# Layer 3's first high parts in layer 2's places, and whole rows' table rows read in pieces

## The chip, the cores and the metric

The kernel runs on one core of a Trainium2 chip. The metric is the device time of one execution in microseconds (us); lower is better. The engines named below are TensorE (PE; its weight loads are PEld), VectorE (DVE), ScalarE (ACT), GpSimd (POOL) and SyncE (SP), which issues most loads and stores.

## What is computed

Four graph layers over 2708 nodes with 512 features. The change touches the end of layer 2 and all of layer 3:

```python
h = jnp.maximum(_layernorm(x), 0.0)
h = relu(adj @ (h @ W1) + b1)             # layer 2, first pass
h = relu(adj @ (h @ W3) + b3)             # layer 2, second pass
x = x + tanh(h @ Wf + bf)

h = jnp.maximum(_layernorm(x), 0.0)       # layer 3
A = (adj != 0)
hidden = h @ W + b                        # 2708 x 512: "the table"
x = x + (A @ hidden) / A.sum(axis=0)[:, None]
```

The adjacency matrix is sparse: its density falls with the node number in both directions, so the first nodes have many neighbours and the last ones few.

## The kernel before

**Tiles.** Nodes are cut into 22 tiles of 128 (the last has 20), and "row m" is the work for the 128 outputs of node tile m. The first six tiles of neighbours (`DENSE = 6`) are taken whole by every row. Of the other 16 a row takes only the neighbours that occur, as lists of 128 found in layer 0: row m has `CHUNKS[m]` of them (9 for row 2, 8 for row 3, 7 for rows 4 to 7, then 6 and 5, and 2 for the short row 21). One indirect DMA of 256 KB on POOL gathers the 128 table rows of one list. Rows 0 and 1 are so dense that layer 3 takes all 22 tiles of neighbours for them ("full rows", `FULL = (0, 1)`).

**Layer 2's second pass** goes over rows 0, 6 to 21, and then 1 to 5. Each row aggregates (lines 946 and 949), projects with `Wf`, applies tanh, adds the residual, normalises, projects with `W`, and stores its part of the table to DRAM as `hid` (line 1240), and from row 6 on to `hidr` as well, from which layer 3 gathers. The six dense tiles' right-hand sides stay in SBUF in three forms, `ghi0..5`, `glo0..5` and `gs0..5`. `gs0` becomes the residual of row 5, the last one.

**Layer 3's ordinary rows** are 2 to 20, with row 21 in the middle (`order_3`). A row's sum is a chain of matmuls into one PSUM bank, of a 0/1 mask on the left and a part of the table on the right. Every table tile is split in two parts that together hold its full precision: a high part by a copy on ACT (line 1073), and a low part by a subtraction on DVE, in place (line 1075). So each tile or list costs two matmuls.

- `hidden(t)` loads dense tile t of the table into `glo{t}` (line 1084) and splits it, with the high part in `ghi{t}`. Both places come free when layer 2's last row has aggregated.
- `gather_h(m)` loads row m's marks (line 1118) and issues its gathers (line 897). Their places come from `room()`: four in `wr`, then eight `gg` places and four of a `wb` weight in turn. Row 2 has the four `wr` places and five `gg`; row 3 three `gg`, four `wb` and one `gg`; row 4 seven `gg`. The `wb` tiles hold the weights of the last projection with `W`.
- `whole_h(m, t0, t1)` makes masks from the marks, three tiles at a time (line 1146), and issues the products with dense tiles t0 to t1.
- `listed_products(m)` makes the lists' masks (line 1157), splits the gathered parts and issues their products. The places of the high parts come from `part_room()`: `v_hi`, `v_lo` and `v_s` in turn, two of each. These are also the places in which layer 2's projections keep the three forms of their left-hand sides.
- `finish_h(m)` scales, adds the residual and stores (lines 1169 and 1172).

Three rows are begun ahead (`AHEAD = 3`): products with the dense tiles 0 to 4 are issued for rows 2, 3 and 4 before any list, and those with tile 5, which layer 2 computes last, behind the row's list. After that every row finishes and starts the one three further on.

**The full rows** are done in steps, one after each ordinary row from the third on: two steps with the dense tiles, six (`others`) with three further table tiles each, and that for rows 0 and 1. These further products are of full-precision operands, not of halves; their table tiles are read by `load_full()`, 16 loads of up to 256 KB (line 1180) into `wa0`, `wa1`, `wa2` and `wr`, issued together in the code after the first ordinary row. The adjacency piece of each step is loaded at line 880 and turned into a 0/1 mask on DVE (line 1191 for dense tiles, 1198 for others).

**Order.** Each engine runs its instructions in a fixed order. The code gives each instruction its priority; a planner makes each engine's order when the kernel is built, taking instructions whose inputs and places it expects to be free by then. So an instruction can run long before its neighbours in the code.

Of the kernel before, what the change touches and what calls it, by code (L numbers as in the profile page):

```python
# [9 lines left out]
FP = mybir.dt.float32  # L10
FR = mybir.dt.float32r
# [11 lines left out]
P = 128  # L23
# [13 lines left out]
DENSE = 6  # L37
# [5 lines left out]
def kernel(  # L43
# [27 lines left out]
    nc = tc.nc  # L71

    N, D = x.shape
    H, _, DK = wk_d.shape
    NT = (N + P - 1) // P
    NFULL = N // P
    TAIL = N - NFULL * P
    NCD = D // P
# [8 lines left out]
    def rows(t):  # L87
        return min(P, N - t * P)

    def dense_of(m):  # L90

        return 0 if m == NT - 1 else DENSE
# [15 lines left out]
    hid = dram.tile([N + 1, D], FP, name="hid")  # L108
# [42 lines left out]
    def span(t):  # L151
        return slice(t * P, t * P + rows(t))
# [8 lines left out]
    def load_w(pool, src, name):  # L161
        w = pool.tile([P, NCD, D], FP, name=name)
        nc.sync.dma_start(out=w, in_=src.rearrange("(c p) k -> p c k", p=P))
        return w

    def norm(pool, xt, n, dst, func=AF.Identity):

        stats = pool.tile([P, nc.vector.BN_STATS_DIM], FP, name="stats")
        nc.vector.bn_stats(stats[:n], xt[:n])
        mv = pool.tile([P, nc.vector.BN_AGGR_DIM], FP, name="mv")  # L170
        nc.vector.bn_aggr(mv[:n], stats[:n])
        rstd = pool.tile([P, 1], FP, name="rstd")
        nc.scalar.activation(rstd[:n], mv[:n, 1:2], AF.Sqrt, bias=eps[:n])
        nc.vector.reciprocal(rstd[:n], rstd[:n])
        shift = pool.tile([P, 1], FP, name="shift")
        nc.vector.tensor_scalar(
            shift[:n], mv[:n, 0:1], rstd[:n], -1.0, op0=ALU.mult, op1=ALU.mult
        )
        nc.scalar.activation(dst[:n], xt[:n], func, scale=rstd[:n], bias=shift[:n])
# [30 lines left out]
    wset = short.enter_context(tc.tile_pool(name="wset", bufs=1))  # L210
# [6 lines left out]
    with tc.tile_pool(name="l0_slab", bufs=2) as slabs, tc.tile_pool(  # L217
        name="l0_h", bufs=1
    ) as hp, tc.tile_pool(name="l0_w", bufs=2) as wp, tc.tile_pool(
        name="l0_acc", bufs=2, space=PSUM  # L220
    ) as ps_acc, tc.tile_pool(name="l0_small", bufs=1, space=PSUM) as ps_small, tc.tile_pool(
        name="l0_list", bufs=3, space=PSUM
    ) as ps_list, tc.tile_pool(name="l0_tr", bufs=1, space=PSUM) as ps_tr, tc.tile_pool(
        name="l0_y", bufs=1, space=PSUM
# [504 lines left out]
        for m in range(NT):  # L729
# [44 lines left out]
            if m == NT // 2 + 2:  # L774
                wr = load_w(wset, w1_d, "wr")
                w1 = split_w(wset, wr, "wa")
                wr = load_w(wset, w3_d, "wr")
# [12 lines left out]
    gp = short.enter_context(tc.tile_pool(name="g", bufs=1))  # L790
    wsetb = short.enter_context(tc.tile_pool(name="wsetb", bufs=1))
    ap = short.enter_context(tc.tile_pool(name="ap", bufs=2))
# [78 lines left out]
    PIECE = 3  # L871
    dense = [list(range(t, min(t + PIECE, DENSE))) for t in range(0, DENSE, PIECE)]
    others = [list(range(t, min(t + PIECE, NFULL))) for t in range(DENSE, NFULL, PIECE)]
# [119 lines left out]
    xs, ys, g1, g1p = {}, {}, {}, {}  # L993
    AHEAD = 9

    def fetch(t):

        n = rows(t)
        xs[t] = gp.tile([P, D], FP, name=f"slot{t % AHEAD}")
        nc.sync.dma_start(out=xs[t][:n], in_=x1[t][:n])  # L1000
        ys[t] = gp.tile([P, D], FP, name=f"slot{AHEAD + t % AHEAD}")
        nc.gpsimd.indirect_dma_start(
            out=ys[t][:n],
            out_offset=None,
            in_=y[:, :],
            in_offset=bass.IndirectOffsetOnAxis(ap=idx[:n, t : t + 1], axis=0),
        )

    def first_product(t):
# [6 lines left out]
        norm(wp, xt, n, hn)  # L1016
        if t + AHEAD < NT:
            fetch(t + AHEAD)
        banks = (ps_a, ("agg", "aggs")) if t % 2 else ()
# [13 lines left out]

    for t in range(min(AHEAD, NT)):
        fetch(t)
    w3 = split_w(wsetb, wr, "wb")
    wr = load_w(wset, wf_d, "wr")

    for m in order_m:
        n = rows(m)  # L1040
        parts = aggregated(m, first_parts, first_product, g1d, bias1, marked=True)
        if m == 0:
            wf = split_w(wset, wr, "wa")
            wr = load_w(wset, w_d, "wr")
# [43 lines left out]
    def room():  # L1088


        quad = wset.tile([P, NCD, D], FP, name="wr")
        for c in range(NCD):
            yield quad[:, c, :]
        i = 0
        while True:
            for _ in range(NGG):
                yield gathered()
            quad = wsetb.tile([P, NCD, D], FP, name=f"wb{i % 3}")
            i += 1
            for c in range(NCD):  # L1100
                yield quad[:, c, :]

    places_h, part_slot = room(), [0]

    def part_room():
        name = ("v_hi", "v_lo", "v_s")[part_slot[0] % 3]
        part_slot[0] += 1
        return wp.tile([P, NCD, P], FR, name=name).rearrange("p c k -> p (c k)")


# [26 lines left out]
    def products_of(m):  # L1137
        return 2 * (dense_of(m) + CHUNKS[m])

    def whole_h(m, t0=0, t1=DENSE):  # L1140

        n = rows(m)
        t1 = min(t1, dense_of(m))
        for ts in (range(t, min(t + PIECE, t1)) for t in range(t0, t1, PIECE)):
            mask = ap.tile([P, PIECE, P], FR, name="a_hi" if t1 - t0 > 1 else "a_s")
            nc.vector.tensor_copy(
                mask[:, : len(ts), :n], marks[m][:, ts[0] : ts[-1] + 1, :n]
            )
            for i, t in enumerate(ts):
                for half in hidden(t):  # L1150
                    add_h(m, mask[:, i, :n], half, products_of(m))

    def listed_products(m):
        n = rows(m)
        whole, num = dense_of(m), CHUNKS[m]
        mask = ap.tile([P, NCA, P], FR, name="ac")[:, :num, :n]
        nc.scalar.copy(mask, marks[m][:, whole : whole + num, :n])
        for c, g in enumerate(listed_h.pop(m)):
            for half in split_h(part_room(), g, P):
                add_h(m, mask[:, c, :], half, products_of(m))  # L1160
# [12 lines left out]

    full_h = {}

    def load_full():
        for i, t0 in enumerate(range(DENSE, NT, NCD)):
            quad = wset.tile([P, NCD, D], FP, name=("wa0", "wa1", "wa2", "wr")[i])
            for t in range(t0, min(t0 + NCD, NT)):
                nc.sync.dma_start(out=quad[: rows(t), t - t0, :], in_=hid[span(t)])  # L1180
                full_h[t] = quad[:, t - t0, :]

    def full_steps(m, name):

        n = rows(m)
        total = 2 * DENSE + sum(map(len, others))
        banks[m] = ps_p.tile([P, D], FP, name=name)
        for t0 in range(0, DENSE, PIECE):
            mask, k = load_piece(m, list(range(t0, t0 + PIECE)))
            high = ap.tile([P, PIECE, P], FR, name="a_lo")  # L1190
            nc.vector.tensor_scalar(high[:, :, :n], mask, 0.0, None, op0=ALU.not_equal)
            for i in range(PIECE):
                for half in hidden(t0 + i):
                    add_h(m, high[:, i, :n], half, total)
            yield
        for ts in others:
            mask, k = load_piece(m, ts)
            nc.vector.tensor_scalar(mask, mask, 0.0, None, op0=ALU.not_equal)
            for i, t in enumerate(ts):
                add_h(m, mask[:k, i, :n], full_h[t][:k], total)  # L1200
            yield
        finish_h(m)


    order_3 = [m for m in range(NT) if m not in FULL and m != NFULL]
# [44 lines left out]


    steps = in_steps()
    AHEAD = 3
    for k in order_3[:AHEAD]:
        if k not in marks:
            gather_h(k)
        whole_h(k, 0, DENSE - 1)
    for i, m in enumerate(order_3):
        listed_products(m)
        if i < AHEAD:  # L1260
            whole_h(m, DENSE - 1)
        finish_h(m)
        if i == 0:
            load_full()
        if i + AHEAD < len(order_3):
            k = order_3[i + AHEAD]
            gather_h(k)
            whole_h(k)
        if i > 1:
            next(steps, None)  # L1270
        if i == 1:
            some = wp.tile([P, 1], FP, name="some", bufs=1)
            nc.vector.tensor_reduce(some, bad, AX.X, ALU.add)
            tot = ps_t.tile([P, 1], FP, name="pt")
            nc.tensor.matmul(tot, ones, some, start=True, stop=True)
            nc.vector.tensor_scalar_min(some, tot, 1.0)
            nc.vector.tensor_copy(flag, some)
# [8 lines left out]
    with tc.If(general > 0):  # L1286

        with tc.tile_pool(name="l0_g", bufs=2) as gp, tc.tile_pool(
            name="l0_gh", bufs=1
# [9 lines left out]
            for m in range(NT):  # L1299
# [23 lines left out]
                for t in range(NT):  # L1323
                    k = rows(t)
# [18 lines left out]
        with tc.tile_pool(name="l1_qkv", bufs=1) as qkvp:  # L1343
# [6 lines left out]
            with tc.tile_pool(name="l1_pw", bufs=1) as pwp, tc.tile_pool(  # L1350
                name="l1_ph", bufs=2
            ) as php, tc.tile_pool(name="l1_px", bufs=3) as pxp, tc.tile_pool(
                name="l1_pps", bufs=2, space=PSUM
# [4 lines left out]
                for w, src in ((wk, wk_d), (wq, wq_d), (wv, wv_d)):  # L1358
                    for h in range(H):
                        nc.sync.dma_start(  # L1360
                            out=w[:, :, h * DK : (h + 1) * DK],
                            in_=src[h].rearrange("(c p) k -> p c k", p=P),
# [34 lines left out]
            with tc.tile_pool(name="l1_bias", bufs=2) as bp, tc.tile_pool(  # L1397
                name="l1_p", bufs=2
            ) as pp, tc.tile_pool(name="l1_pT", bufs=3) as ptp, tc.tile_pool(
                name="l1_x", bufs=1  # L1400
            ) as xp, tc.tile_pool(name="l1_st", bufs=4) as stp, tc.tile_pool(
                name="l1_s", bufs=2, space=PSUM
            ) as ps_s, tc.tile_pool(name="l1_t", bufs=2, space=PSUM) as ps_t, tc.tile_pool(
                name="l1_o", bufs=1, space=PSUM
            ) as ps_o, tc.tile_pool(name="l1_y", bufs=1, space=PSUM) as ps_y:
                SW = 2 * BLK
                for m in range(NT):
# [11 lines left out]
                    for h in range(H):  # L1419
# [23 lines left out]
                        for t0 in range(0, NT, 4):  # L1443
                            ts = range(t0, min(t0 + 4, NT))
                            pt = ps_t.tile([P, 4, P], FP, name="pt")
                            pT = ptp.tile([P, 4, P], FP, name="pT")
                            for t in ts:
                                k = rows(t)
# [9 lines left out]
                            for t in ts:  # L1458
                                k = rows(t)
# [29 lines left out]
        with ExitStack() as gen:  # L1489
# [8 lines left out]
            gp = l2.enter_context(tc.tile_pool(name="g", bufs=2))  # L1498
# [213 lines left out]
```

## Time and profile before

| | us |
|---|---|
| median of 7 runs | 1485.69 (1481.43 to 1491.27) |
| the profiled execution | 1490.49 |
| its span, first to last instruction | 1488.7 |
| PE / DVE / ACT / POOL busy in the span | 1305.7 / 940.1 / 676.9 / 668.4 |
| layer 3's gathers on POOL (all places) | 120, at a median of about 0.95 each |
| ACT cast to a high part, line 1073 | 0.62 |
| DVE subtraction, line 1075 | 0.69 |

The profiled execution lies 4.8 us above the median and within the range of the runs. A busy PE is not PE at its peak; the granted clock has to be read beside it. In the timelines below, a row gives the start, the duration (for several instructions in one row their whole stretch), the engine, the line, the operation, destination and source by the program's names with buffer numbers left out, the count, and in brackets the engine's idle time before it and what ended that.

### The profile page before, as it was taken

To read this page: it belongs to the slowest core of one execution; us is meant where nothing else is said; L and a number is where in the kernel's file an instruction comes from. 1 tells how busy PE (TensorE), PEld (TensorE's weight loads), DVE (VectorE), ACT (ScalarE), POOL (GpSimd) and SP (SyncE) were. 2 spreads that over 40 slices of the span, in tenths; PEclk is the share of its full clock that TensorE was granted. 3 is DMA by queue.
4 is the path that set the end of the run, shared out by engine and by line. 5 is a ranking of instruction groups with operands and counts; after the bars stand their busy time and mean duration, and the time that the engine had idled before them with its cause. 6 is when DMAs were issued, how large, how long until landed. Compare 5 with 4: busy or idle time off the path is not lost. (4 is left out here: it accounts for less than half of the span.)

```text
span 1488.7 us, 15398 instructions
## 1 busy us (share of the span) xinstructions
PE 1305.7 (88%) x4400; PEld 771.6 (52%) x4400; DVE 940.1 (63%) x1888; ACT 676.9 (45%) x1040; POOL 668.4 (45%) x690
## 2 busy tenths in 40 slices
PE   5487889779778769989999999899999999778997
PEld 2133334334333346656656666465676666456664
DVE  2578877978879679543334446465666665565664
ACT  5998545453111256432232335244445444454543
POOL 1263667556553332055544441334424345157762
PEclk9699999889889879999999999999999999879998
DMA  8999999887696497378776777756555666478874
GB/s 290 330 342 310 336 309 308 298 254 214 207 327 226 145 316 246 103 228 268 246 234 210 237 228 229 247 158 196 177 172 161 209 198 205 122 245 260 265 238 143
DMA packets 195941, 351.27 MB, mean 236 GB/s; under 512 B 26445, under 2 KB 107693, under 8 KB 192114
## 3 DMA queue, kind: packets, MB, share of 16 engines
q1 hardware_dynamic: 148453, 200.68, 40.3%
q0 software_dynamic: 47392, 149.51, 32.1%
q8 instruction: 37, 0.61, 0.2%
q14 instruction: 59, 0.48, 0.1%
HBM read 286.99 MB, written 63.12 MB: 235 GB/s over the span
## 5 line engine op out<-in xcount | busy, mean ns | idle before, releaser
L949 PE MATMUL aggs<-gg,ac 128*128 128x512 f32 (+1 forms) x520 | 232.5, 595 | 4.6 <-DMA gg<-g1d,idx_g 4.6
L897 POOL DMA_INDIRECT gg<-g2d,idx_g x130 | 130.9, 1007 | 218.4 <-PE aggs L949 169.2
L897 POOL DMA_INDIRECT gg<-g1d,idx_g x130 | 132.4, 1019 | 176.5 <-PE aggs L949 106.0
L741 PE MATMUL acc<-h,inc 128*128 128x512 f32 x348 | 168.5, 627 | 26.5 <-DVE inc L600 23.9
L532 POOL DMA_INDIRECT ac<-in_adj_t_dram,idx_a x130 | 130.6, 1004 | 87.8 <-issue 32.6
L949 PEld LDWEIGHTS aggs<-gg,ac 128*128 128x128 f32 (+1 forms) x520 | 97.8, 189 | 111.2 <-issue 101.0
L550 POOL DMA_INDIRECT h<-h0d,idx_g x111 | 111.7, 1006 | 90.4 <-PE acc L741 66.6
L741 PEld LDWEIGHTS acc<-h,inc 128*128 128x128 f32 x348 | 66.0, 199 | 105.9 <-issue 70.5
L946 PE MATMUL agg<-ghi,a_hi 128*128 128x512 f32 x252 | 115.6, 459 | 3.0 <-ACT a_hi L933 2.7
L933 ACT ACTIVATE a_hi<-raw 128x384 fp32r<-128x384 f32 x84 | 43.5, 519 | 163.1 <-issue 86.7
L741 PE MATMUL acc<-h,incl 128*128 128x512 f32 (+1 forms) x222 | 105.3, 621 | 0.0
L946 PE MATMUL agg<-glo,a_lo 128*128 128x512 f32 x252 | 102.1, 405 | 1.5 <-ACT glo L200 1.5
L946 PE MATMUL aggs<-gs,a_s 128*128 128x512 f32 x252 | 100.6, 402 | 0.7 <-DVE gs L197 0.6
L897 POOL DMA_INDIRECT gg<-hidr,idx_h x79 | 78.6, 995 | 48.6 <-PE agg L1133 16.9
L934 DVE TENSOR_TENSOR a_lo<-raw,a_hi 128x384 fp32r<-128x384 f32 x84 | 47.3, 563 | 77.9 <-ACT a_hi L933 51.2
L157 PE MATMUL yacc<-wvo,hT 128*128 128x512 f32 (+1 forms) x176 | 87.4, 643 | 4.6 <-ACT hT L186 4.5
L843 DVE SCALAR_TENSOR_TENSOR v_lo<-pt,v_hi 128x512 fp32r<-128x512 f32 (+1 forms) x88 | 56.6, 664 | 45.9 <-ACT v_hi L842 45.3
L824 DVE SCALAR_TENSOR_TENSOR u<-aggs,u 128x512 f32<-128x512 f32 x42 | 28.9, 687 | 77.2 <-PE aggs L949 75.6
L741 PEld LDWEIGHTS acc<-h,incl 128*128 128x128 f32 (+1 forms) x222 | 43.5, 199 | 53.8 <-issue 51.6
L483 ACT ACTIVATE sgn<-ar 128x2708 bf16<-128x2708 f32 (+1 forms) x22 | 54.0, 2454 | 35.7 <-DMA ar<-in_adj_dram 35.2
L842 ACT ACTIVATE v_hi<-pt 128x512 fp32r<-128x512 f32 (+1 forms) x88 | 48.6, 578 | 43.9 <-PE pt L837 41.8
L514 DVE FIND_INDEX8 at_top<-top,ar 128x8 uint32<-128x2708 f32 (+1 forms) x22 | 65.3, 2969 | 0.0
(275 smaller groups left out, 2774.2 us busy)
## 6 DMA issues: line engine op xcount, KB each, us to landing
ar<-in_adj_dram SPq DMA_DIRECT2D x27, 1354.0 KB
raw<-in_adj_t_dram SPq DMA_DIRECT2D x108, 192.0 KB
slot<-x SPq DMA_DIRECT2D x41, 256.0 KB
at<-in_adj_t_dram SPq DMA_DIRECT2D x27, 384.0 KB
ranks<-rank_b SPq DMA_DIRECT2D x20, 485.0 KB
ac<-lst SPq DMA_DIRECT2D x16, 384.0 KB
h<-in_x_dram SPq DMA_DIRECT2D x21, 256.0 KB
h0d<-h POOLq DMA_DIRECT2D x21, 256.0 KB, 6.0
```

The lines of the kernel that those rows point to most:

```text
L157: nc.tensor.matmul(acc[:n], hT[:, c, :n], w[:, c, :], start=(c == 0), stop=(c == NCD - 1))
L483: nc.scalar.activation(sgn[:n], ar[:n], AF.Sign, accum_out=sum_sgn[:n])
L514: nc.vector.max_index(at_top[:n], top[:n], ar[:n])
L532: nc.gpsimd.indirect_dma_start(out=ac[:, c, :n], out_offset=None, in_=adj_units, in_offset=bass.IndirectOffsetOnAxis(ap=idx_a[:, m, c0 + c ...
L550: nc.gpsimd.indirect_dma_start(out=g, out_offset=None, in_=h0d[:, :], in_offset=bass.IndirectOffsetOnAxis(ap=idx_g[:, m, c : c + 1], axis=0),)
L741: nc.tensor.matmul(acc[:n], a, g, start=(i == 0), stop=(i == len(pairs) - 1))
L842: nc.scalar.activation(hi[d], pt[d], AF.Relu, scale=UP)
L843: nc.vector.scalar_tensor_tensor(lo[d], pt[d], 0.0, hi[d].bitcast(FP), op0=ALU.max, op1=ALU.subtract)
L897: nc.gpsimd.indirect_dma_start(out=gs[c], out_offset=None, in_=gd[:, :], in_offset=bass.IndirectOffsetOnAxis(ap=index[:, m, c : c + 1], ax ...
L934: nc.vector.tensor_tensor(lo[d], raw, hi[d].bitcast(FP), ALU.subtract)
L946: nc.tensor.matmul(acc[:n], a[:k, i, :n], b[:k], start=st, stop=sp)
L949: nc.tensor.matmul(mixed[:n], a, g, start=(c == 0 and not dense_of(m)), stop=(c == len(chunks) - 1),)
```

## The change

Four edits.

1. `part_room()`: the first 14 high parts (nine of row 2, five of row 3) go to `gs1` to `gs5` in turn. From then on every other part goes there and the others to `v_hi`, `v_lo` and `v_s`, so that there are eleven places instead of six.
2. Row 2's listed products come first of layer 3, ahead of any product with a dense tile. For the other rows they stay where they were.
3. For the first three rows the dense tiles 4 and 5 are late, instead of tile 5 alone (`LATE = 2`). The name of the mask follows: `a_s` for the late piece, `a_hi` otherwise.
4. `load_full(ts)` is called by the full rows' steps: each asks for its own table tiles and the next step's, if they aren't there yet. The places are as before.

```diff
+    NFIRST = 14
+
     def part_room():
-        name = ("v_hi", "v_lo", "v_s")[part_slot[0] % 3]
+        i = part_slot[0]
         part_slot[0] += 1
+        if i < NFIRST or i % 2:
+            return gp.tile([P, D], FR, name=f"gs{1 + (i if i < NFIRST else i // 2) % (DENSE - 1)}")
+        name = ("v_hi", "v_lo", "v_s")[i // 2 % 3]
         return wp.tile([P, NCD, P], FR, name=name).rearrange("p c k -> p (c k)")
...
-            mask = ap.tile([P, PIECE, P], FR, name="a_hi" if t1 - t0 > 1 else "a_s")
+            mask = ap.tile([P, PIECE, P], FR, name="a_s" if t0 else "a_hi")
...
-    def load_full():
-        for i, t0 in enumerate(range(DENSE, NT, NCD)):
-            quad = wset.tile([P, NCD, D], FP, name=("wa0", "wa1", "wa2", "wr")[i])
-            for t in range(t0, min(t0 + NCD, NT)):
-                nc.sync.dma_start(out=quad[: rows(t), t - t0, :], in_=hid[span(t)])
-                full_h[t] = quad[:, t - t0, :]
+    quads = {}
+
+    def load_full(ts):
+        for t in ts:
+            i, j = divmod(t - DENSE, NCD)
+            if t in full_h:
+                continue
+            if i not in quads:
+                name = ("wa0", "wa1", "wa2", "wr")[i]
+                quads[i] = wset.tile([P, NCD, D], FP, name=name)
+            full_h[t] = quads[i][:, j, :]
+            nc.sync.dma_start(out=full_h[t][: rows(t)], in_=hid[span(t)])
...
-        for ts in others:
+        for j, ts in enumerate(others):
+            load_full(sum(others[j : j + 2], []))
             mask, k = load_piece(m, ts)
...
-    AHEAD = 3
-    for k in order_3[:AHEAD]:
+    AHEAD, LATE = 3, 2
+    for i, k in enumerate(order_3[:AHEAD]):
         if k not in marks:
             gather_h(k)
-        whole_h(k, 0, DENSE - 1)
+        if i == 0:
+            listed_products(k)
+        whole_h(k, 0, DENSE - LATE)
     for i, m in enumerate(order_3):
-        listed_products(m)
+        if i:
+            listed_products(m)
         if i < AHEAD:
-            whole_h(m, DENSE - 1)
+            whole_h(m, DENSE - LATE)
         finish_h(m)
-        if i == 0:
-            load_full()
```

## The prediction

> **What bounds the kernel now.** I read the page first, then a table of busy time by stage, then the timelines of TensorE (PE), ScalarE (ACT), SyncE (SP) and GpSimd (POOL) around the seam between layer 2's last row and layer 3, since every edit lies there or later. The page's chain of waits covers only the last 17 us and tells nothing of the change. The page's first line:
>
> ```profile
> PE 1305.7 (88%) x4400; PEld 771.6 (52%) x4400; DVE 940.1 (63%) x1888; ACT 676.9 (45%) x1040; POOL 668.4 (45%) x690
> ```
>
> PE is the fullest engine, but an average hides where it isn't. Stages of layer 3 (stage, its length, busy us of PE, PEld, DVE, ACT, POOL, granted clock, DMA share, GB/s):
>
> ```profile
> 1300.00:1314.00 14.00, 7.54 (x22) 5.36 (x23) 6.96 (x15) 7.06 (x11) 0.00 (x0) 0.63 0.73 248
> 1314.00:1330.00 16.00, 10.92 (x49) 8.68 (x48) 10.49 (x18) 9.13 (x17) 12.62 (x12) 0.97 0.76 250
> 1330.00:1345.00 15.00, 12.32 (x41) 9.65 (x41) 8.06 (x17) 7.39 (x14) 11.34 (x13) 0.80 0.80 242
> 1345.00:1375.00 30.00, 26.64 (x97) 19.89 (x98) 18.34 (x33) 13.12 (x22) 23.30 (x23) 0.92 0.82 256
> 1375.00:1437.00 62.00, 59.98 (x219) 40.57 (x217) 41.97 (x77) 30.95 (x54) 46.32 (x47) 0.98 0.87 276
> ```
>
> From 1375 PE is 97% busy and sets the pace. Between 1300 and 1375 PE is busy 57.4 of 75 us, and POOL does nothing before 1314. The hole is there. PE's waits in it (start, length, idle before and its releaser in brackets):
>
> ```profile
> 1306.46 0.79 PE L1133 MATMUL agg<-ghi,a_hi 128*128 128x512 f32 x1 [6.75 <-ACT ghi L1073]
> ...
> 1330.15 0.80 PE L1133 MATMUL agg<-ghi,a_s 128*128 128x512 f32 x1 [5.23 <-ACT ghi L1073]
> ...
> 1371.34 0.50 PE L1133 MATMUL aggs<-v_lo,ac 128*128 128x512 f32 x1 [2.18 <-ACT v_lo L1073]
> ```
>
> The first two wait for table tiles 4 and 5, the last to be computed; the third for a gathered row. ACT shows what held them:
>
> ```profile
> 1305.79 0.62 ACT L1073 CAST ghi<-glo 128x512 fp32r<-128x512 f32 x1 [3.89 <-DMA glo<-hid]
> ...
> 1328.96 0.62 ACT L1073 CAST v_lo<-gg 128x512 fp32r<-128x512 f32 x1 [2.81 <-DMA gg<-hidr,idx_h]
> 1329.48 0.61 ACT L1073 CAST ghi<-glo 128x512 fp32r<-128x512 f32 x1
> ```
>
> Tile 4 waits for its own load. Tile 5's cast has no idle time: it stands in ACT's queue behind a cast that waited for a gather. SP:
>
> ```profile
> 1301.31 0.32 SPq L1084 DMA_DIRECT2D glo<-hid  x1
> 1301.73 4.38 SPq L1180 DMA_DIRECT2D wa<-hid  x8
> ...
> 1317.88 1.28 SPq L1180 DMA_DIRECT2D wr<-hid  x3
> 1320.10 0.32 SPq L1084 DMA_DIRECT2D glo<-hid  x1
> ```
>
> Tile 4's load (`glo<-hid`) follows four of `load_full`'s 256 KB loads and took 4.5 us (1301.31 to 1305.79); two earlier ones, issued at 1267.54 and 1284.63, took 2.7 and 2.6. Tile 5's follows three more. POOL:
>
> ```profile
> 1275.55 0.95 POOL L897 DMA_INDIRECT gg<-hidr,idx_h  x1 [0.30 <-issue]
> 1314.02 1.33 POOL L897 DMA_INDIRECT wb<-hidr,idx_h  x1 [37.52 <-issue]
> ...
> 1366.14 0.95 POOL L897 DMA_INDIRECT gg<-hidr,idx_h  x1 [0.30 <-PE main L1133]
> ```
>
> POOL idles 37.5 us: its next place is `wb`, the weights of the last row's last product. Then it issues 40 gathers to the one at 1366.14, 52.1/39 = 1.34 us apart, and that one's landing (about 1370.7) ends PE's third wait. So 1314 to 1371 is a chain of POOL issues.
>
> **What the Trainium skill says.** "Perfetto Trace Analysis", Tensor Engine Instruction, says that ACT, DVE and GpSimd are strict first-in first-out; the cast at 1329.48 agrees. "DMA: Bandwidth & Descriptors", Queues, rings and completion order, says that descriptors are taken in ring order within a queue and that an engine takes turns between queues; the 4.5 against 2.6 us agree. "TensorE: Matmul & The Clock Gate", Part 1, says that an idle window of about 3.4 us halves the clock; after each of the two long waits the matmuls start 0.43 us apart instead of 0.23.
>
> **The change, part by part.** *The order on each engine.* It is planned when the kernel is built, and the planner moves ready work far ahead: layer 3's first marks load (L1118) runs at 891.8, before layer 2's second pass, and two of the third stage's pieces are already turned into masks (L1198) at 1273 and 1275, 90 us before their use at 1364. I assume the same afterwards.
>
> *Table rows in pieces.* The same 16 loads, no byte less. Twelve go to `wa`, free at 1297.9, and SP has nothing else to send: later in the code is not later in time here. I take them as unmoved: 0. If they do move, tile 4 lands in 2.6 instead of 4.5 us: -1.9; and the first of the steps, which then asks for six rows (1.5 MB, at the 250 GB/s shown 6 us), could wait up to +4. The four in `wr` can start once row 2's first four products are done, now before the seam: they leave tile 5's way. On SP they then stand ahead of row 4's or 5's store of `hid`: if PE comes to row 2 later than planned, that store waits with them; bounds 0 and +2, I take 0.
>
> *Row 2's listed products first, in the places of layer 2's right-hand sides.* They move 9 casts (0.62), 9 subtractions (0.69) and 18 matmuls. `gs1` to `gs5` are last read at 1265.85 (L946); row 2's gathers, the last of them issued at about 1272, land by 1277; the mask is cast at 1256. Today the casts start at 1311.31, when `v_hi` to `v_s` come free of the last row. Now all fits before 1306. PE: 18 x 0.23 = 4.1 us into the waits of 6.75, 2.68 and 1.28 us at 1299, 1285 and 1290: hidden. With five places for nine parts, the sixth cast waits for PE's first product, and behind it on ACT wait the last row's casts and activations. On ACT and DVE all 18 stand among the last row's own steps. I take two casts on its path, +1.0; bounds 0 and +4.5, where one casts waits for a gather's landing (4.5 median) ahead of a step of the row. The filled wait keeps the clock up for the last row's matmuls: -0.5 (ten matmuls between 1306.5 and 1312 started 0.43 apart, 2 us, of which little is on the path).
>
> *POOL's head start.* Row 2 frees five `gg` places. They are those of row 3's last gather and row 4's first four, so five gathers go into the 37.5 us in which POOL idles and come out of the chain behind 1314: 5 x 1.34 = -6.7. If row 3's first three products, whose gathers have landed too and which are among the first 14 parts, also run before 1314, three more go: -10.7. I take -6.7, since these stand behind the late tiles in the code.
>
> *LATE = 2.* Tile 4's products move behind row 2's list for all three first rows. Today row 4's mask for tiles 0 to 2 waits for a place held until tile 4 arrives (masks at 1308.02 and 1308.87); with tile 3 alone in the second piece, row 4's 8 matmuls can fill the first wait too. No instruction is added: the late mask covers two tiles instead of one. 26 x 0.23 = 6.0 us of cover against 6.75. Counted with POOL, since PE has slack: 0; bounds -2 and 0.
>
> *Tile 5's wait.* 5.23 us plus the slow matmuls after it are PE slack before 1371, not a second gain: the gathers end last there. Less traffic by the `wr` loads shortens the landings (5.2 us for that of 1323.71 against 4.5): -0.7.
>
> *Eleven places for parts instead of six, later.* ACT can cast five parts further ahead. From 1375 PE is the bound and a part that is ready sooner gains nothing; 0, bounds -3 (PE's idle time after 1375 on parts) and +14 (below).
>
> Sum: 1.0 - 0.5 - 6.7 - 0.7 = -6.9, call it -7. From 1371 on PE carries the lead to the end: the same products follow in the same order. The profiled execution took 1490.49 us around a span of 1488.7, so it would take about 1483.5; it lies 4.8 above the median of 1485.69, and from that the change gives 1478.7.
>
> **Rivals.** *A, more is gained: 1472.* Eight gathers move, tile 4's wait shrinks: -10.7 - 1.9 - 0.7 = -13. For it: PE's slack between 1300 and 1371, about 17.6 us, allows it. Against: needs row 3 early.
>
> *B, the loads really spread: 1476.* -7 - 1.9, minus or plus the step's wait. Against it: the marks at 891.8.
>
> *C, the lead is lost: 1484.* The planner still sends the `wb` gathers first, as now (seven of them at 1314), and row 4's wait behind them; or the lead is spent at the next place: row 7's last `gg` places are freed by row 6's products, and from 1358.56 on most `gg` gathers are released by PE, not by POOL itself. Only the landings and a part of the seam stay: -2.
>
> *D, slower: 1493.* ACT and DVE, first-in first-out, park at gathers of rows further ahead, and masks, subtractions and finishes of nearer rows stand behind. Between 1314 and 1375 ACT already waits 19.2 us for gathers, and PE's waits for masks (`a_hi`) are 8.0 us in 5, 1.6 each. With eleven places the plan lets ACT pass the point where six now hold it. One such wait in every second of 18 rows is 0.8 x 18 = 14.4, less the 7. It cancels the gain from 0.39 us a row, and makes the kernel slower by 4.5 us from 0.64. Against: in PE's stage gathers land ahead of need, and PE's longest wait for a part there is 0.53 us.
>
> **How the numbers follow.** Forecast 0.42, A 0.12, B 0.08, C 0.18, D 0.20. 0.3% is 4.5 us, about what can be told from no change. Faster: A, B and 0.40 of the forecast, 0.60. Same: C and the forecast's edge, 0.20. Slower: D, 0.20. The range takes A with its own spread at the low end (1468) and C and the cheaper half of D at the high end (1490); the likeliest case alone is 1474 to 1481.
>
> **What would show it.** Right: `wr` and `wb` loads aside, POOL issues about five gathers between 1276 and 1314; row 2's matmuls (`gs` as moving operand) before 1306; no 5 us wait at tile 5; the last row's product ends within 1 us of 1315; twelve `wa<-hid` loads still in one bunch near 1298. Wrong: POOL's idle time stays above 35 us (C); PE's waits for `a_hi` or parts grow behind 1345 (D); the last row's product ends past 1320.

## The result, and the profile after

The changed kernel is slower: a median of 1495.38 us (1488.69 to 1504.72, 25 runs) against 1486.01 us (62 runs) for the kernel before on the same chip. The ratio is 1.0067, with a 95% interval of 1.0051 to 1.0083. Its profiled execution took 1499.09 us around a span of 1497.2. Edits 1 and 4 add lines, so the changed kernel's lines below have higher numbers than before: products are L1140 (L1133 before), masks L1153 (L1146), finishes L1176 (L1169), table loads L1194 (L1180).

Busy time by stage in the changed kernel (columns as in the table of the prediction, with the granted clock behind POOL's busy time):

```profile
1300.00:1314.00 14.00, 8.00 (x34) 5.86 (x32) 7.42 (x12) 4.71 (x7) 1.26 (x2) 0.98 0.53 155
1314.00:1330.00 16.00, 9.45 (x29) 6.71 (x29) 6.07 (x14) 6.37 (x10) 2.60 (x3) 0.59 0.43 149
...
1375.00:1437.00 62.00, 58.34 (x201) 39.83 (x202) 40.35 (x75) 30.42 (x52) 47.84 (x45) 0.92 0.85 264
1437.00:1455.00 18.00, 12.66 (x38) 7.96 (x37) 9.17 (x17) 6.94 (x12) 5.48 (x6) 0.81 0.51 161
```

The last of these stages in the kernel before:

```profile
1437.00:1455.00 18.00, 15.92 (x50) 11.38 (x51) 9.28 (x19) 7.14 (x13) 6.85 (x8) 0.81 0.58 173
```

PE issues 18 fewer matmuls between 1375 and 1437 than before (201 against 219; it enters this stage some 3 us later), and between 1437 and 1455 it is only 70% busy, where it was 88%. Its long waits (timeline of PE, changed kernel):

```profile
1319.21 0.79 PE L1140 MATMUL agg<-ghi,a_s 128*128 128x512 f32 x1 [10.09 <-ACT ghi L1073]
...
1374.38 0.50 PE L1140 MATMUL aggs<-gs,ac 128*128 128x512 f32 x1 [2.38 <-ACT gs L1073]
...
1418.98 0.69 PE L1140 MATMUL agg<-ghi,a_hi 128*128 128x512 f32 x1 [1.88 <-DVE a_hi L1153]
...
1449.57 0.80 PE L1140 MATMUL agg<-ghi,a_hi 128*128 128x512 f32 x1 [5.34 <-DVE slot L1176]
```

There are two places of loss. The first is the seam: 10.09 us for tile 4, where the kernel before waited 6.75. The second lies in the stage in which I had PE set the pace: behind 1385, 3.0 us of waits for masks (`a_hi`), 0.5 before, and 5.34 us for a row's finish (`slot`), which is what frees a PSUM bank. The kernel before already waited for that finish, but less:

```profile
1439.08 0.79 PE L1133 MATMUL agg<-ghi,a_hi 128*128 128x512 f32 x1 [2.89 <-DVE slot L1169]
```

The second place is the larger in these two executions: from PE's wait at 1371.34 to the end of the span the kernel before took 117.4 us, and from that at 1374.38 the changed kernel took 122.8.

ACT at the seam:

```profile
1309.67 0.63 ACT L1238 ACTIVATE u<-u 128x512 f32<-128x512 f32 x1 [0.64 <-DVE u L1237]
1318.02 0.62 ACT L1073 CAST gs<-gg 128x512 fp32r<-128x512 f32 x1 [7.72 <-DMA gg<-hidr,idx_h]
1318.54 0.61 ACT L1073 CAST ghi<-glo 128x512 fp32r<-128x512 f32 x1
1319.17 1.28 ACT L173 ACT_TABLE_LOAD   x1
```

The cast at 1318.02 belongs to row 4's list. Behind it in ACT's queue stand the cast of tile 4 (1318.54) and the last row's normalisation. POOL shows when its gather was issued:

```profile
1277.61 0.95 POOL L897 DMA_INDIRECT gg<-hidr,idx_h  x1 [0.30 <-issue]
1282.03 0.94 POOL L897 DMA_INDIRECT gg<-hidr,idx_h  x1 [3.48 <-DVE gg L1075]
...
1309.39 1.06 POOL L897 DMA_INDIRECT gg<-hidr,idx_h  x1 [9.19 <-PE aggs L1140]
1326.79 0.95 POOL L897 DMA_INDIRECT wb<-hidr,idx_h  x1 [16.34 <-issue]
```

That gather went out at 1309.39, and its cast could start 8.6 us later. SP shows which loads were issued right behind it:

```profile
1309.58 0.32 SPq L1084 DMA_DIRECT2D glo<-hid  x1
1310.00 5.71 SPq L1194 DMA_DIRECT2D wa<-hid  x8
```

The head start that I predicted is there, and larger: 20 of layer 3's gathers have gone out before the first one into `wb`, against 12 before, seven of them from 1282 to 1309, in the time in which POOL idled 37.5 us. But the `wb` gathers start at 1326.79 instead of 1314.02, since the last row now ends later. Eight gathers ahead at 1.34 us are 10.7 us; the later start is 12.8. That leaves a loss of 2.1 us, and PE's wait at 1374.38 comes 3.0 us later than that at 1371.34 before.

DVE ahead of the wait for the finish (changed kernel):

```profile
1438.22 0.69 DVE L1075 TENSOR_TENSOR gg<-gg,gs 128x512 fp32r<-128x512 f32 x1 [1.87 <-ACT gs L1073]
1438.83 0.35 DVE L1153 CAST a_hi<-nz 128x384 fp32r<-128x384 uint8 x1
1440.85 0.69 DVE L1075 TENSOR_TENSOR gg<-gg,v_hi 128x512 fp32r<-128x512 f32 x1 [1.66 <-ACT v_hi L1073]
1443.75 0.69 DVE L1075 TENSOR_TENSOR gg<-gg,gs 128x512 fp32r<-128x512 f32 x1 [2.21 <-ACT gs L1073]
1444.36 0.35 DVE L1153 CAST a_hi<-nz 128x384 fp32r<-128x384 uint8 x1
...
1446.35 0.69 DVE L1075 TENSOR_TENSOR gg<-gg,v_s 128x512 fp32r<-128x512 f32 x1 [1.04 <-ACT v_s L1073]
...
1448.77 0.74 DVE L1176 SCALAR_TENSOR_TENSOR slot<-agg,rdeg,slot 128x512 f32<-128x512 f32 x1
```

PE's last product of that row began at 1442.12. Its finish ran 6.7 us later, behind six subtractions of the next rows' gathered parts and a mask. Two of the six (1443.75 and 1446.35) waited for a cast on ACT that waited for its gather; the others were ready, and took DVE 0.7 us each. The two masks shown stand behind such waiting subtractions too.

What ACT's casts waited for between 1376 and 1450 us (idle time before them in us, number of times), in the kernel before:

```profile
  PE agg L1133: 19.0, 5
  DMA gg<-hidr,idx_h: 11.2, 10
  PE aggs L1133: 6.3, 2
  DVE gg L1075: 0.8, 1
```

and in the changed kernel:

```profile
  DMA gg<-hidr,idx_h: 36.1, 25
  DMA gg<-hid,idx_g: 1.5, 1
```

With six places ACT mostly waits for PE to give a place back, so it stays in step with PE. With eleven, all the waiting that is listed is for gathers that have not landed. ACT's waiting didn't shrink (37.3 us listed before, 37.6 after); it moved from the places to the gathers.

### The profile page after: what moved, and what is told of

Read it like the earlier page. It is cut to its first block, busy times and chain, and to the rows that moved or that the text cites. A ratio compares the mean times of both kernels' runs of the same rounds, so it can differ in the third digit from the quotient of the medians.

```text
span 1497.2 us, 15352 instructions
## 1 busy us (share of the span) xinstructions
PE 1305.0 (87%) x4400; PEld 768.6 (51%) x4400; DVE 940.5 (63%) x1888; ACT 678.0 (45%) x1040; POOL 676.8 (45%) x690
## 5 line engine op out<-in xcount | busy, mean ns | idle before, releaser
L897 POOL DMA_INDIRECT gg<-hidr,idx_h x79 | 83.4, 1056 | 74.9 <-PE agg L1140 24.9
L512 DVE MAX8 top<-ar 128x8 f32<-128x2708 f32 (+1 forms) x22 | 65.3, 2970 | 0.0
```

The costliest lines, as they stand in the source:

```text
L512: nc.vector.max(top[:n], ar[:n])
L897: nc.gpsimd.indirect_dma_start(out=gs[c], out_offset=None, in_=gd[:, :], in_offset=bass.IndirectOffsetOnAxis(ap=index[:, m, c : c + 1], ax ...
```

## The experiments

Three mechanisms are told apart. **S**: a cast of row 4 stands on ACT ahead of the last row's steps, at the seam. **P**: eleven places for parts put casts, and with them subtractions, ahead of masks and finishes later (the prediction's rival D). **L**: the table loads, sent in a bunch beside tile 4's load and the gather, make these late. Ratios are to the kernel before on the same chip; the runs were spread over several chips.

A trace shows one execution. That of six took 1489.72 us against its median of 1483.29, that of held 1481.64 against 1491.64. The kernel pieces below keeps the order of the kernel before, and yet its last row of layer 2 ends 53 us behind row 5's last product with a dense tile, where that of the kernel before ends 49 us behind. So a difference of some 3 us at the seam between two traces tells nothing by itself; the ratios do. PE's waits for masks and for the finish behind 1385 differ by less in these two: 0.2 and 2.65 us in pieces, 0.5 and 2.89 before.

| run | ratio | 95% interval |
|---|---|---|
| the change | 1.0067 | 1.0051 to 1.0083 |
| pieces (edit 4 alone) | 1.0005 | 0.9976 to 1.0034 |
| places (edit 1 alone) | 1.0089 | 1.0064 to 1.0114 |
| late1 | 1.0029 | 1.0008 to 1.0049 |
| six | 0.9968 | 0.9946 to 0.9990 |
| six_late1 | 0.9981 | 0.9964 to 0.9998 |
| held | 1.0038 | 1.0018 to 1.0058 |
| six_held | 0.9946 | 0.9925 to 0.9966 |
| six_held_banks | 0.9946 | 0.9926 to 0.9965 |
| notfirst | 1.0052 | 1.0030 to 1.0075 |
| eleven_early | 1.0011 | 0.9993 to 1.0030 |
| eleven_late | 1.0069 | 1.0050 to 1.0089 |
| banks | 1.0022 | 1.0001 to 1.0043 |
| masks | 1.0051 | 1.0029 to 1.0072 |
| banks_masks | 1.0009 | 0.9985 to 1.0033 |
| six_masks | 1.0024 | 0.9995 to 1.0053 |

**late1: tile 4 no longer late.** `LATE = 1` has tile 5 alone late again, as in the kernel before.

```diff
-    AHEAD, LATE = 3, 2
+    AHEAD, LATE = 3, 1
```

> The changed kernel with one edit undone: only tile 5 is late, tile 4's products stand ahead again; eleven places for parts stay. Theory S (the seam): in the changed kernel a cast of row 4's list stood on ACT ahead of tile 4's cast and of the last row's normalisation, and waited 7.7 us for its gather; here that cast comes behind them, so PE's wait of 10.1 us shrinks to 4 or less, the last row's product ends about 8 us sooner, and the kernel takes about 1488 (ratio to before 1.001). Theory P (eleven places delay masks and finishes in later rows): unchanged at about 1495 (1.006), with PE's waits for masks and finishes from 1376 on still near 8 us.

The cast of row 4 is no longer ahead at the seam, where PE waits 6.55 us for tile 4, as before. The ratio is 1.0029, so S, or what else late tiles and eleven places do together, is worth some 0.4% in the changed kernel. But PE still waits 4.4 us for masks and 7.33 us for a finish behind 1385: there is a second cause.

**six: six places from the 15th part on.** The rest of the change stays.

```diff
-        if i < NFIRST or i % 2:
+        if i < NFIRST:
...
-        name = ("v_hi", "v_lo", "v_s")[i // 2 % 3]
+        name = ("v_hi", "v_lo", "v_s")[i % 3]
```

> The changed kernel with six places for parts (v_hi, v_lo, v_s in turn) from the 15th part on; the first 14 stay in gs1 to gs5. Theory S: row 4's parts have no place before the last row is done, so the cast that waited 7.7 us is gone from the seam: about 1487 (1.001) from that alone. Theory P: the masks and finishes of later rows come in time again, PE waits for them 3.5 us instead of 8: about 1490 (1.003) from that alone. Both: 1482 to 1484, 0.998.

At 0.9968 this is faster than both kernels. PE's waits:

```profile
1316.45 0.80 PE L1140 MATMUL agg<-ghi,a_s 128*128 128x512 f32 x1 [4.97 <-ACT ghi L1073]
...
1372.36 0.80 PE L1140 MATMUL aggs<-v_lo,ac 128*128 128x512 f32 x1 [5.21 <-ACT v_lo L1073]
...
1441.55 0.50 PE L1140 MATMUL agg<-ghi,a_hi 128*128 128x512 f32 x1 [0.97 <-DVE slot L1176]
```

The wait for a finish falls to 0.97 us and those for masks are gone. The eleven places thus cost about 1.0% (1.0067 less 0.9968), some 15 us, and all else together gains 0.3%, 4.8 us.

**held: the table loads held back.** A copy of one element from a row finished about three rows before stands ahead of each load, so that the bunch leaves the seam (the loads then run from 1340 us on).

```diff
...
             full_h[t] = quads[i][:, j, :]
+            done = finished[-4] if len(finished) > 3 else finished[0]
+            nc.vector.tensor_copy(full_h[t][:1, :1], done[:1, :1])
             nc.sync.dma_start(out=full_h[t][: rows(t)], in_=hid[span(t)])
```

> The changed kernel with the full rows' 16 table loads truly held back: one element of each place is first copied on DVE from the result of a row finished about three rows earlier, so no load can start at the seam. Theory L (traffic): the gather of row 4 landed 8.6 us after its issue because twelve 256 KB loads were under way; without them 4.5 us, tile 4's load 2.6: the last row's product ends 4 to 7 us sooner, about 1489 (1.003). Theory S without L: the order on ACT is what counts, the cast's wait remains at about the landing of a gather, 3 to 4 us: within 2 us of the changed kernel. If the held loads come too late for the first full step, PE waits there up to 6 us.

The wait for tile 4 falls to 3.10 us. ACT at the seam (held):

```profile
1301.39 0.62 ACT L1073 CAST ghi<-glo 128x512 fp32r<-128x512 f32 x1 [1.25 <-DMA glo<-hid]
1302.80 0.62 ACT L1073 CAST gs<-gg 128x512 fp32r<-128x512 f32 x1 [0.79 <-DMA gg<-hidr,idx_h]
```

The gather of row 4, issued at 1299.24, now takes 3.6 us instead of 8.6: L is there. But tile 4's cast also comes ahead of row 4's here, so that this run takes away a part of S with L and can't tell how much of the seam is L. The ratio, 1.0038, still leaves the kernel slower.

**pieces: edit 4 alone, on the kernel before.**

> The kernel before with the fourth edit alone: table rows asked for by the full rows' steps, one step ahead. The prediction took it at nothing, since loads are planned as soon as their places are free whatever their place in the code: ratio 1.000, the twelve loads still in one bunch near 1298, the four others near 1318. If the code's order counts: the loads spread from about 1340 on, tile 4's load lands 1.9 us sooner, ratio 0.998 or less.

No difference that can be told: 1.0005. Every engine runs its instructions in the same order as before, so the order in the code that this edit changes isn't the order of execution.

**places: edit 1 alone, on the kernel before.**

> The kernel before with the places for parts alone changed (first 14 in gs, then eleven), nothing of the row order, the pieces or LATE. None of layer 3's casts stands ahead of the last row's steps on ACT, so theory S gives no loss at the seam. Theory P: PE's waits behind 1376 us on masks (a_hi) or on parts grow as in the changed kernel, the stretch from the end of the last row's product to the last finish takes as in late1 or after, 160 to 164 us against six's 153, and the ratio is 1.004 (1.001 to 1.007). Theory that eleven places cost only through the casts at the seam: 1.000 (0.998 to 1.002), no wait for a_hi over 0.5 us behind 1376.

This is the clearest run. Without any other part of the change the eleven places make the kernel 0.9% slower, 13 us, more than I expected of P, and at the seam PE waits for tile 4 as before (6.53 us). PE's later waits:

```profile
1416.26 0.51 PE L1137 MATMUL agg<-gs,ac 128*128 128x512 f32 x1 [2.24 <-ACT gs L1073]
1424.55 0.80 PE L1137 MATMUL agg<-ghi,a_hi 128*128 128x512 f32 x1 [2.52 <-DVE a_hi L1150]
1453.19 0.80 PE L1137 MATMUL agg<-ghi,a_hi 128*128 128x512 f32 x1 [6.60 <-DVE slot L1173]
```

The mask that PE waits for at 1424.55 was not behind a subtraction that waited. DVE waited for a full row's adjacency piece there:

```profile
1423.26 0.36 DVE L1202 TENSOR_SCALAR raw<-raw 128x384 f32<-128x384 f32 x1 [2.86 <-DMA raw<-in_adj_t_dram]
1423.54 0.69 DVE L1075 TENSOR_TENSOR gg<-gg,gs 128x512 fp32r<-128x512 f32 x1
1424.14 0.35 DVE L1150 CAST a_hi<-nz 128x384 fp32r<-128x384 uint8 x1
```

So loads that land late can hold the masks too. In the stage from 1376 to 1450 DVE's waits for loads of pieces and marks add up to nothing in the kernel before, 2.8 us in six, 3.5 in the changed kernel and 4.7 in places. Why they land late I didn't test. The delay reaches POOL as well, which from 1314 to 1438 had issued without a pause over 2 us in the kernel before:

```profile
1429.83 3.02 POOL L897 DMA_INDIRECT wb<-hidr,idx_h  x1 [4.51 <-DVE gg L1075]
```

If POOL waits for DVE there, as this line has it, while DVE waits for ACT and ACT for POOL's next gather, a delay can go round. The changed kernel doesn't need such a ring: POOL has no wait over 1.1 us between 1376 and 1450 there.

**six_late1: both suspects out.** six with LATE = 1.

> The changed kernel with both suspected costs taken out: six places for parts from the 15th on, and tile 3 back in the first piece of the first three rows (LATE = 1). Theory S (a cast of row 4's list that waits for its gather on ACT, ahead of the last row's steps, costs the seam) and theory P (eleven places let ACT take casts in an order that PE waits for later): six has already taken both out, since none of row 4's casts is ahead of tile 4 there, so LATE adds nothing: ratio to the kernel before 0.997 (0.994 to 1.000), as six, and 0.006 under late1. Theory that LATE = 2 is itself worth something (row 4's early products fill PE's wait for tile 4): 1.000, with PE's wait for tile 4 at 6.5 us instead of six's 5.0. Theory that LATE = 2 costs something by itself (its first piece stands ahead): 0.994.

(What comes back ahead of the lists is tile 4.) 0.9981; its interval overlaps six's, so LATE by itself is worth nothing that can be told. S needs both edits: where row 2's list comes first, a cast of row 4 comes ahead of tile 4's with LATE = 2 and eleven places; with either alone it doesn't.

**six_held and six_held_banks.** six with the loads held, by copies from rows of layer 3 as in held; then with the six banks described below.

> six with the sixteen table rows' loads held until a row of layer 2 finished about three rows before has been copied, as in held. Theory L (tile 4's and tile 5's loads are late because the twelve loads into wa run beside them): PE's wait for tile 4 falls from 5.0 us to about 3, ratio 0.995 (0.992 to 0.998). Theory that the seam is set by the row's own chain once row 4's casts are out of it: as six, 0.997, wait 5 us. Theory that the held loads come too late for row 3's or 4's whole-row products: PE waits for DVE or SP behind wa, 1.001.

> six_held (0.9946) with the same six banks. It waited 1.0 us for a slot in layer 3, so on either theory the gain is at most 1 us: 0.994 (0.991 to 0.997). If the two further banks let the planner take the next rows' masks ahead of nearer work, it is slower: 0.998.

Both come to 0.9946, about 8 us under the kernel before; the interval overlaps six's, so what the held loads add is likely but not certain. PE's wait at the seam falls to 2.39 us. No cast of row 4 is ahead there in six either, so this is L alone: tile 4's load takes 2.7 us instead of 4.5 (six_held):

```profile
1303.10 0.65 PE L1140 MATMUL agg<-ghi,a_s 128*128 128x512 f32 x1 [2.39 <-ACT ghi L1073]
```

**notfirst: row 2's list not first.** The other edits stay.

> The changed kernel without taking row 2's listed products first; places, pieces and LATE as changed. On ACT casts of row 2's list, whose gathers landed near 1277, then stand ahead of tile 4's cast, and none of row 4's, so theory S gives no wait of 7.7 us there. POOL's head start is lost with it (its idle time is back at over 30 us) unless row 2's casts still end before 1306. Theory S plus P: end of the last row's product within 52 us of row 5's last product (the changed kernel 61, before 49), ratio 1.003 (1.000 to 1.006), by P. Theory that row 2's list first caused the loss at the seam by itself, by filling ACT and DVE: as S. Theory that LATE or the places caused it whatever order the rows have: 60 us again, ratio 1.007.

1.0052, within the expected range: P is there (waits for masks of 6 us behind 1385, 5.07 us for a finish). At the seam the last row's end comes 57 us behind row 5's last product with a dense tile, between the expected 52 and the changed kernel's 61, so this run doesn't settle what row 2's list does there. POOL's head start stays: 20 gathers are out before the first one into `wb`.

**eleven_early and eleven_late: where the eleven places cost.** Eleven places for the lists of rows 2 to 7 alone (up to the 45th part), and from row 8 on alone.

```diff
-        if i < NFIRST or i % 2:
+        if i < NFIRST or (i < NLIST and i % 2):
...
-        name = ("v_hi", "v_lo", "v_s")[i // 2 % 3]
+        name = ("v_hi", "v_lo", "v_s")[(i // 2 if i < NLIST else i) % 3]
```

(NLIST is 45; eleven_late has `i >= NLIST` in both.)

> The changed kernel with eleven places for parts up to the 45th (the lists of rows 2 to 7, used up to about 1376 us) and six from there on. Theory P-late (eleven places cost in TensorE's stage behind 1376, where subtractions of later rows' gathers stand ahead of masks and finishes on DVE): most of the loss between six (0.997) and the changed kernel (1.007) goes except the seam's wait of 10 us for tile 5, of which little reaches the end: 0.999 (0.996 to 1.002), and no wait for a_hi over 1 us behind 1385. Theory P-early (the casts of row 4 on ACT ahead of the last row's steps, and what they delay up to 1376, are the loss): 1.005.

> The changed kernel with six places for parts from the 15th to the 45th and eleven behind that: the reverse of eleven_early. Theory P-late: ratio 1.004 (1.001 to 1.008), the seam as in six (wait for tile 5 of about 5 us), waits for a_hi and a wait for a row's finish (slot) of 4 us or more between 1385 and 1455. Theory P-early: as six, 0.997, and a wait for slot of about 1 us.

(Both texts say tile 5 for the wait at the seam; it is tile 4.) P holds, and for the late lists: eleven_late alone has the whole loss (1.0069), though its seam is as good as six's; eleven_early has row 4's cast ahead of tile 4's, as the changed kernel, and is at 1.0011. eleven_early:

```profile
1313.65 0.80 PE L1140 MATMUL agg<-ghi,a_s 128*128 128x512 f32 x1 [7.36 <-ACT ghi L1073]
...
1436.52 0.50 PE L1140 MATMUL agg<-ghi,a_hi 128*128 128x512 f32 x1 [1.31 <-DVE slot L1176]
```

eleven_late:

```profile
1308.83 0.80 PE L1140 MATMUL agg<-ghi,a_s 128*128 128x512 f32 x1 [5.26 <-ACT ghi L1073]
...
1443.84 0.79 PE L1140 MATMUL agg<-ghi,a_hi 128*128 128x512 f32 x1 [6.95 <-DVE slot L1176]
```

The two parts don't add up: their losses against six are 0.4% and 1.0%, and both together 1.0%.

What ACT's casts waited for between 1376 and 1450 us goes with this. In eleven_early and six, where PE's wait for a finish is short, ACT waited 13.8 and 15.0 us for gathers, and 22.5 and 20.6 us for places. In eleven_late and the run places it waited 35.3 and 35.4 us for gathers, and 7.0 and 0.5 us for places.

**banks, masks, banks_masks, six_masks: how the loss reaches PE.** The changed kernel with six PSUM banks instead of four for the rows' sums; with four places for the dense tiles' masks instead of two; with both; and six with four mask places.

```diff
-            banks[m] = ps_a.tile([P, D], FP, name=("agg", "aggs")[len(opened) % 2])
+            pool, name = ((ps_a, "agg"), (ps_a, "aggs"), (ps_t, "pt"))[
+                len(opened) % (2 if len(opened) < 6 else 3)
+            ]
+            banks[m] = pool.tile([P, D], FP, name=name)
...
-            mask = ap.tile([P, PIECE, P], FR, name="a_s" if t0 else "a_hi")
+            mask = ap.tile([P, PIECE, P], FR, name="a_s" if t0 or (t1 == DENSE and ts[0]) else "a_hi")
```

> The changed kernel with six PSUM banks for the ordinary rows' sums instead of four, from the seventh row begun on (the two that layer 2 used for its transposes are free then). It takes away TensorE's wait for a finish (slot, 5.3 us in the changed kernel), not the place of the finish in DVE's queue. Theory that the finish behind other rows' subtractions is what costs: 1.003 (1.000 to 1.005), no wait for slot. Theory that it is one face of DVE's and ACT's being parked at gathers, and TensorE would wait for the next mask or part instead: 1.006 to 1.008, with waits for a_hi or gs of together 4 us or more in the place of that for slot.

> The changed kernel with four places for the dense tiles' masks instead of two from row 5 on: the second piece goes to a_s. Theory (a), masks and finishes behind subtractions on DVE: waits for a_hi behind 1385 (2.7 us in the changed kernel) go, the one for slot stays, 1.005 (1.003 to 1.007). Theory (b), late parts: 1.007, as the changed kernel, with the waits moved to gs and v_ parts.

> The changed kernel with six banks and four mask places. Theory (a): 0.998 (0.995 to 1.001), near six (0.997), with waits for masks and for slot behind 1385 of under 2 us together. Theory (b): 1.002 or more, as banks alone, with waits for gs and v_ parts in the place of the 7.4 us for a_hi there.

> six (0.997) with four mask places, as a control. It waited 0.6 us for a mask in layer 3 and 1.0 for a slot, so either theory says 0.997 (0.994 to 0.999). If more mask places gain something whatever the parts do, it is 0.993 or less, and the gain of banks_masks can't be put down to (a).

Two more banks take away the wait for a finish and about half of the loss (1.0022), but the waits for masks grow from 3.0 to 7.4 us:

```profile
1414.30 0.50 PE L1143 MATMUL agg<-ghi,a_hi 128*128 128x512 f32 x1 [2.73 <-DVE a_hi L1156]
1418.40 0.50 PE L1143 MATMUL agg<-ghi,a_hi 128*128 128x512 f32 x1 [2.45 <-DVE a_hi L1156]
...
1442.31 0.50 PE L1143 MATMUL aggs<-ghi,a_hi 128*128 128x512 f32 x1 [2.17 <-DVE a_hi L1156]
```

The first two of these masks stand behind waits of DVE for adjacency pieces (1.70 and 2.07 us), the third behind a subtraction that waited. More mask places alone do little (1.0051, overlapping the change). With both the ratio is 1.0009, just inside the range expected if masks and finishes on DVE carry the loss (theory (a)), but the waits are not gone as that theory had it: 7.0 us for masks stay, and DVE's longest wait is now for a load of marks (banks_masks, DVE):

```profile
1429.17 0.52 DVE L1156 CAST a_hi<-nz 128x384 fp32r<-128x384 uint8 x1 [4.26 <-DMA nz<-nz]
```

And the control went against my expectation: four mask places make six slower, 1.0024, with 5.1 us of waits for finishes. The trace shows why it may: with places free, DVE comes to the masks before their marks have landed, and waits 16.8 us for marks in six waits between 1376 and 1450, where it waited 2.8 us once in six. It is the same pattern on another engine.

Of the 1.0% between six and the change, banks_masks takes away 0.6 (1.0067 to 1.0009), although its mask places bring such waits with them (9.9 us for marks). So masks and finishes that come late from DVE carry over half of the loss, by the medians. How much of their lateness is due to subtractions that waited and how much to late loads isn't settled, and neither is what carries the rest; the traces show only that each place that is added moves the wait to the next one.

## Why the prediction was wrong

The forecast was -6.9 us; the change brought about +10. Step by step:

- **"Eleven places for parts instead of six, later": the step that failed.** It said that PE is the bound from 1375 on and "a part that is ready sooner gains nothing; 0, bounds -3 (PE's idle time after 1375 on parts) and +14". places measured +13 us, the edge of the bound. The gain was rightly seen as none; the cost was taken as none because PE's longest wait for a part was 0.53 us. That is PE's side, and not all of it: its longest wait behind 1375, 2.89 us for a finish at 1439.08, was left out. The side to read was ACT's: 25.3 us of waiting for places beside 11.2 us for gathers. The places were what kept ACT and DVE in step with PE. POOL was issuing nearly all the time from 1314 to 1438, so parts could hardly come sooner, and the freed ACT could only go and wait at a gather, with masks and finishes behind the subtractions that DVE does after ACT's casts.
- **Rival D** named this mechanism, with 1493 us, and it has come nearest to the 1495.4 measured. The number is luck in part. Its 8.0 us in 5 waits for masks is a sum over the whole of layer 3 that counts PE's waits and those of its weight loads for the same masks; PE itself waited once between 1314 and 1375, 2.9 us, and 0.5 us later. Two more points of it were off. Its price was for masks from 1345 on, but between 1345 and 1385 PE's waits for them didn't grow (2.9 us before, 3.0 after), and behind 1385 the longest wait is for a finish that holds a bank. And its counter-argument, that gathers land ahead of need there, spoke of PE's need and not of ACT's.
- **"I take two casts on its path, +1.0; bounds 0 and +4.5"** was mis-sized. One cast waited 7.72 us, past the bound; I took a median landing of 4.5 us for a gather that lands amid table loads. Measured from row 5's last product with a dense tile in layer 2 (1265.85 before, 1267.06 after) the last row's end moved from 49 to 61 us behind it, +12. That one cast is not all of it. In eleven_early, banks, masks and banks_masks, which have it too, it waited 5.0 to 5.5 us, PE waited 7.4 to 7.8 us for tile 4, and the last row ended 57 to 60 us behind; in six and eleven_late, which don't have it, PE waited 5.0 and 5.3 us, and the row ended 57 and 54 us behind. What else delays the last row isn't settled. late1 (51 us at the seam) is 0.4% or 6 us faster than the change, so some half of the 12 us reaches the end.
- **POOL's head start**, -6.7 for five gathers, was right in kind: eight went ahead, as rival A had it (-10.7), and the later seam took it back. With six places from the 15th part on (six) the change gains 4.8 us, with an interval of 1.5 to 8.0 that contains the forecast's 6.9. So the rest of the sum stands as a whole, not term by term: two errors, the head start that was larger and the last row that ends later (57 us behind in six too), go against each other, and that is luck.
- **Table rows in pieces**, 0: right, pieces shows it. The four `wr` loads went ahead of the seam as said, and the twelve `wa` loads stayed in a bunch.
- **LATE = 2**, 0: right by itself (six against six_late1). That it would let row 4's casts ahead, together with the places, I missed.
- **The smaller terms**, -0.5 for the clock and -0.7 for tile 5's wait, had no run of their own. The wait for tile 5 is gone; the granted clock between 1314 and 1330 fell to 0.59, where it was 0.97.
- **The rule that a lead at 1371 is carried to the end** was wrong as well: with eleven places from row 8 on alone (eleven_late) the seam is as in six, and 1.0% is lost behind it.

## What to carry to other kernels

A buffer that is too scarce to run far ahead can be what keeps an in-order engine near the work that is due. Before adding places, read what the engine that fills them waits for: if it is a place, ask what it will wait for next and what stands behind it in its queue; if the source is itself at its limit, more places may give nothing, and what is queued behind can come late. And try a change of several edits with each one alone: here a part of one edit of four held the whole loss, and without that part the rest gains.

## What the runs showed that I had not expected

- A gather of 256 KB, 4.5 us at the median from issue to landing, took 8.6 us in the changed kernel, where eight loads of 256 KB were issued right behind it. With the same loads behind it it took 5.9 to 6.2 us in eleven_early, banks and masks, and with the loads held, 3.6.
- After PE's wait of 10.09 us and two short ones, four matmuls `main<-wb,v_hi` took 2.07 us together (1323.97), where the same four took 1.08 in the kernel before (1312.20). The granted clock of the 16 us from 1314 on was 0.59.
- One indirect issue on POOL took 3.02 us (places, 1429.83) and one 5.03 (eleven_late, 1419.07), where most take 0.95.
- More mask places, which only allow work to be done sooner, made six slower, from 0.9968 to 1.0024.
